# The first attention's projection as seven half-size products instead of eight

## The chip, the cores and the metric

The kernel runs on one core of a Trainium2 chip. The metric is the device time of one launch in microseconds, less is better. One profiled execution of the kernel before gives the rows that the text reads.

## The reference

Sixteen batches of a graph with 1024 nodes and 256 features go through two layers. Cut to what matters:

```python
h = maximum(layernorm(x), 0)
# layer 0
out = relu(h @ mlp1_w + mlp1_b)                 # [1024, 512]
residual = out
hf = out @ W_fc                                  # [1024, 512]: the projection that is changed
e = leaky_relu(f1[:, None] + f2[None, :], 0.2)   # f1 = hf @ a_fc[:512], f2 = hf @ a_fc[512:]
out = elu(elu(softmax(e) @ hf)) + residual       # dense attention, no mask
out = relu(out @ mlp2_w + mlp2_b)                # [1024, 256]
residual = out
out = elu(gat(out, adj, W_hand, a_hand)) + residual   # masked attention "a"
x = x + relu(out)
# layer 1
h = maximum(layernorm(x), 0)
x = x + relu(gat(h, adj, W, a, slope=0.01))      # masked attention "b"
```

All data is float32. The projection is, per batch, a product of 1024 x 512 by 512 x 512.

## The kernel before, in words

A batch's 1024 nodes are eight row tiles of 128. The activations `resT` are held with features on the partitions, in four blocks of 128 features; `wfc_sb` holds W_fc in two halves of 256 output columns, each with one more column that gives f1 or f2. `Dense.project(t, g)` (L754 to L767) multiplies row tile t by half g: four products of 128 x 128 weights by 257 columns are accumulated in one PSUM bank (L762), ScalarE copies the bank into `h_nat` (L764), and for half 0 GpSimd takes the f1 column out and writes ones in its place (L766, L767). Sixteen such calls make a batch.

The first attention has no mask, and is done without a 1024 x 1024 matrix for all batches but part of the first: the nodes are ranked by f2 (`rank`), their rows of `h_nat` scattered to DRAM in that order (`scatter`, GpSimd's indirect DMA), read back (`read_sorted`), and running sums made in both directions (`sum_before`, `sum_behind`). The sums are written as tables, each node gathers its row by its f1 (`gather`), and `share` and `mean` make the result `hp` of it. `merge` (L1001) transposes `hp` on TensorE and applies the two elu, `merge_end` adds it to `resT`, `mlp2` multiplies by mlp2_w. The two masked attentions (`Masked`: "a" and "b" in tile names) build 128 x 256 weights on VectorE (L667) in a ring of eight tiles with the tag "att", and multiply them (L677).

Engines work in the order of the program. That order is written out: `at(name, lo, hi, steps)` gives each step a nominal time, `SHIFT` moves single steps, and at the end all steps are sorted by that time and issued. TensorE, VectorE, ScalarE and SyncE take their instructions in that order, and GpSimd's are chained in it too, the scatters in between free among themselves. A period of 142 nominal units stands for one batch; `base_of(b)` is where batch b's begins. Several batches are in flight: while batch b is in its second masked attention, batch b + 1 ends its first one and batch b + 2 is projected. `dense_rows` places half 1 of the projection, `dense_begin` half 0 with the columns, the ranks and the scatters.

Tiles come from rings. `mm_psum` has four banks, `bc_psum` one tile of two banks, `tr_psum` two banks. The tag "seq" has two large buffers, taken in turn by `h_nat`, the sorted rows `xs`, the running sums `tt` and the two halves of the gathered rows `got`. A tile that is taken waits until the last user of its buffer is done.

## Time and profile before

| | |
|---|---|
| median of 3 runs | 2252.64 us (2251.83 to 2252.95) |
| the profiled execution | 2251.37 us |
| its span, first to last instruction | 2249.6 us |
| granted TensorE clock | 0.998 |
| LDWEIGHTS of the projection (L762) | 2048, 189 ns each |
| copies of its banks (L764, ScalarE) | 256 |
| HBM read and written | 226.88 MB and 126.29 MB |

A row of a group names line, engine, operation and tiles, then how many, the busy time in us and the mean length of one in ns, and the idle time of its engine just before, with what ended it. PE is TensorE's matmul, PEld its weight load, DVE VectorE, ACT ScalarE, POOL GpSimd, SP SyncE. A row of a stage (A:B) has the stage's length and then the busy time and number of instructions of PE, PEld, DVE, ACT and POOL. A row of waits has the us in total, how many, and the longest.

### The profile page before, as it was taken

What the parts mean: (1) busy time and instruction counts of PE and PEld (TensorE: products, weight loads), DVE (VectorE), ACT (ScalarE), POOL (GpSimd) and SP (SyncE); (2) the same over time, 40 slices, a digit from 0 to 9 for tenths busy, and PEclk for the clock granted to TensorE, in tenths of its full rate; (3) what the DMA queues carried; (4) which work ended last, traced back from release to release, by engine and by line L of the source; (5) the groups of instructions that cost most, each with busy time, mean ns of one, the idle gap of its engine ahead of it and who ended that gap; (6) DMA issues with size and microseconds to landing.
All of it is one profiled execution on the core that took longest, in us unless ns stands there. A gap on an engine that the chain in (4) does not pass through costs nothing.

```text
span 2249.6 us, 31025 instructions
## 1 busy us (share of the span) xinstructions
PE 2207.2 (98%) x9754; PEld 1723.4 (77%) x9754; DVE 1643.1 (73%) x4535; ACT 1259.6 (56%) x2797; POOL 954.4 (42%) x1212
## 2 busy tenths in 40 slices
PE   7999999999999999999999999999999999999997
PEld 5767777787877878787787877878787787877776
DVE  7677676777867678776776867677786776858765
ACT  5355745547365564756557375564746557365542
POOL 1163425263452536425263452636435263543620
PEclk9999999999999999999999999999999999999999
DMA  5568466675766757566685666757566585645700
GB/s 197 159 175 196 114 208 154 186 183 148 197 123 200 187 168 190 137 196 148 192 191 147 189 127 194 188 177 189 130 205 144 185 197 153 164 125 169 178 22 28
DMA packets 263870, 368.95 MB, mean 164 GB/s; under 512 B 124352, under 2 KB 175880, under 8 KB 259600
## 3 DMA queue, kind: packets, MB, share of 16 engines
q1 hardware_dynamic: 217088, 202.72, 31.9%
q0 software_dynamic: 45952, 163.99, 28.9%
q8 instruction: 80, 1.31, 0.3%
q14 instruction: 94, 0.77, 0.1%
q10 hardware_dynamic: 656, 0.17, 0.0%
HBM read 226.88 MB, written 126.29 MB: 157 GB/s over the span
## 4 chain that ended last, share of the span: by engine, by line
PE 75%; DVE 6%; DMA 2%; POOL 2%; ACT 1%; issue 1%; POOLq 0%; DVEq 0%; ACTq 0%; SPq 0%
PE oa L677 17%; PE h L762 16%; PE ob L677 14%; PE m L1024 8%; PE m L748 6%; PE pa L614 4%; PE pb L614 3%; PE hpT L1006 2%; DMA got<-coarse,k 2%; DVE attb L667 1%; PE carry L918 1%; PE on L1038 1%; PE nt L536 1%; DVE stats L516 1%; DVE hp L959 1%
## 5 line engine op out<-in xcount | busy, mean ns | idle before, releaser
L677 PE MATMUL ob<-hmb,attb 128*128 128x257 f32 x2048 | 463.9, 380 | 2.2 <-DVE attb L667 1.9
L762 PE MATMUL h<-wfc_sb,resT 128*128 128x257 f32 x2048 | 462.8, 379 | 0.0
L677 PE MATMUL oa<-hma,atta 128*128 128x258 f32 x2048 | 459.9, 382 | 1.8 <-DVE atta L667 1.5
L677 PEld LDWEIGHTS ob<-hmb,attb 128*128 128x128 f32 x2048 | 383.9, 190 | 67.2 <-issue 12.3
L677 PEld LDWEIGHTS oa<-hma,atta 128*128 128x128 f32 x2048 | 384.8, 190 | 59.3 <-DVE atta L667 2.9
L762 PEld LDWEIGHTS h<-wfc_sb,resT 128*128 128x128 f32 x2048 | 380.1, 189 | 59.1 <-issue 7.4
L705 POOL TENSOR_TENSOR posa<-posa,onat 128x256 f32<-128x256 f32 x118 | 106.7, 904 | 546.1 <-ACT posa L693 487.6
L667 DVE SCALAR_TENSOR_TENSOR attb<-rowsb,qwdb,edge 128x256 f32<-128x256 f32 (+1 forms) x536 | 292.1, 563 | 34.6 <-PE ob L677 28.6
L667 DVE SCALAR_TENSOR_TENSOR atta<-rowsa,qwda,edge 128x256 f32<-128x256 f32 (+1 forms) x520 | 257.3, 524 | 51.4 <-DMA rowsa<-row_a 35.6
L934 POOL DMA_INDIRECT got<-coarse,k x124 | 203.4, 1640 | 90.9 <-DMA got<-fine,k 56.6
L748 PE MATMUL m<-hT,w_sb 128*128 128x512 f32 x512 | 236.6, 596 | 1.9 <-ACT rb L719 1.1
L1024 PE MATMUL m<-resT,w_sb 128*128 128x512 f32 x512 | 228.3, 593 | 1.0 <-POOL resT L1017 1.0
L719 ACT ACTIVATE rb<-ob,recb 128x256 f32<-128x256 f32 x128 | 58.5, 474 | 274.9 <-DVE recb L717 248.9
L1017 POOL TENSOR_TENSOR resT<-resT,e 128x512 f32<-128x512 f32 x128 | 165.5, 1295 | 104.9 <-DVE e L1016 96.7
L692 ACT ACTIVATE ea<-oa,reca 128x256 f32<-128x256 f32 x128 | 60.3, 471 | 248.1 <-DVE reca L689 228.7
L934 POOL DMA_INDIRECT got<-fine,k x124 | 126.7, 1022 | 128.5 <-DVE hpd L999 41.9
L1024 PEld LDWEIGHTS m<-resT,w_sb 128*128 128x128 f32 x512 | 94.5, 190 | 102.4 <-issue 93.5
L748 PEld LDWEIGHTS m<-hT,w_sb 128*128 128x128 f32 x512 | 94.2, 191 | 89.0 <-issue 74.7
L822 POOL DMA_INDIRECT sorted<-hnat,place x128 | 128.6, 1004 | 53.9 <-DVE place L815 33.0
L764 ACT COPY hnat<-h 128x257 f32<-128x257 f32 x256 | 90.8, 367 | 104.1 <-PE h L762 101.6
L845 ACT ACTIVATE junk<-r,fs 128x1024 int8<-128x1024 f32 x124 | 142.6, 1150 | 0.9 <-POOL fs L766 0.6
L1016 DVE SCALAR_TENSOR_TENSOR e<-hpT,e 128x512 f32<-128x512 f32 x128 | 87.9, 688 | 53.2 <-ACT e L1010 53.0
(195 smaller groups left out, 3391.2 us busy)
## 6 DMA issues: line engine op xcount, KB each, us to landing
xs<-sorted SPq DMA_DIRECT2D x32, 1028.0 KB
fine<-tt SPq DMA_DIRECT2D x32, 1026.0 KB
fine<-xs SPq DMA_DIRECT2D x32, 1026.0 KB
x<-in_x_dram SPq DMA_DIRECT2D x16, 1024.0 KB
xn<-in_x_dram SPq DMA_DIRECT2D x15, 1024.0 KB
out_dram<-x SPq DMA_DIRECT2D x28, 512.0 KB
hT<-xn SPq DMA_DIRECT2D x416, 32.0 KB
coarse<-carry SPq DMA_DIRECT2D x32, 256.5 KB
```

Source lines behind the costliest of these rows:

```text
L614: nc.tensor.matmul(ps[:, :2 + F], lhsT=hT[:, c, t * P:(t + 1) * P], rhs=self.w_sb[:, c, 0, :], start=(c == 0), stop=(c == FC - 1))
L667: nc.vector.scalar_tensor_tensor(a_t[:, :n * P], self.rows[:, i], self.qwd[:, 1, j:j + 1], edge[:, j, i], op0=OP.max, op1=OP.mult)
L677: nc.tensor.matmul(self.out[t][:, :F + self.ONES], lhsT=self.att[t0, j][:, (t - t0) * P:(t - t0 + 1) * P], rhs=self.hm[:, j, 2:2 + F + sel ...
L705: adder.tensor_add(pos, pos, o_nat[:, t, :])
L748: nc.tensor.matmul(ps, lhsT=w1_sb[:, kc, c * P:(c + 1) * P], rhs=piece(kc, h), start=(kc == 0), stop=(kc == FC - 1))
L762: nc.tensor.matmul(ps[:, :F + 1], lhsT=self.resT[:, kc, t * P:(t + 1) * P], rhs=wfc_sb[:, kc, g, :], start=(kc == 0), stop=(kc == HC - 1))
L764: nc.scalar.copy(self.h_nat[:, t, g, :], ps[:, :F + 1])
L822: made = nc.gpsimd.indirect_dma_start(out=sorted_d[self.b % 2], out_offset=bass.IndirectOffsetOnAxis(ap=self.place[:, t:t + 1], axis=0), i ...
L845: nc.scalar.activation(junk, self.r2, AF.Sign, bias=self.fs[:, 0, t:t + 1], accum_out=self.signs[:, t:t + 1])
L934: nc.gpsimd.indirect_dma_start(out=got[u // n][:, u % n, :], out_offset=None, in_=(coarse_d if coarse else fine_d)[self.b % 2][:, :], in_o ...
L1017: nc.gpsimd.tensor_add(dst, dst, e)
L1024: nc.tensor.matmul(ps, lhsT=w2_sb[:, kc, c * P:(c + 1) * P], rhs=self.resT[:, kc, h * HALF:(h + 1) * HALF], start=(kc == 0), stop=(kc == H ...
```

## The change

The projection C = A B is cut into halves in all three dimensions, and the four blocks of C are made from seven products of half size instead of eight (Strassen's method in Winograd's form). A11, A12 are the upper 512 rows with feature blocks 0, 1 and 2, 3; A21, A22 the lower 512 rows. The sums of weight blocks are made once at the start (`seven_weights`, on GpSimd): the buffers of `wfc_sb` are overwritten by them, `wfc_more` holds two more, and B21 itself goes to DRAM and is loaded in each batch into two tiles of the attention ring. The sums of activation blocks are made per row tile, two on VectorE and two on GpSimd, also in that ring. Products 1, 6, 5 and 3 of a row tile accumulate in one PSUM bank, which is copied after each of them; product 7 of two row tiles goes to the two banks of `bc_psum` and is added to two blocks by `add_pair`; products 2 and 4 go to a bank each and are added by VectorE.

```diff
+    wfc_more = const.tile([P, 2, 2, F + 1], F32, name="wfc_more")
+    wfc_d = dram.tile([P, 2 * (F + 1)], F32, name="wfc_d")
+    def seven_weights():
+        top, low = slice(0, 2), slice(2, HC)
+        b11, b12, b21, b22 = [wfc_sb[:, k, g, :] for k in (top, low) for g in range(2)]
+        nc.sync.dma_start(wfc_d.rearrange("p (k f) -> p k f", k=2), b21)
+        nc.gpsimd.tensor_sub(wfc_more[:, 1], b22, b12)
+        nc.gpsimd.tensor_sub(b12, b12, b11)
+        nc.gpsimd.tensor_sub(wfc_more[:, 0], b22, b12)
+        nc.gpsimd.tensor_sub(b21, b21, wfc_more[:, 0])
...
+    def att_tile(name):
+        return big.tile([P, F + 1], F32, tag="att", name=name, bufs=ATT)
...
-        def project(self, t, g):
+        def sums_of(self, u, which):
...
+            a11, a12 = self.resT[:, 0:2, one], self.resT[:, 2:HC, one]
+            a21, a22 = self.resT[:, 0:2, two], self.resT[:, 2:HC, two]
+            t = self.s[which, u] = att_tile(f"s{which}_{self.b}_{u}")[:, :PAIR].rearrange(
+                "p (k n) -> p k n", k=2)
+            if which == 1:
+                nc.vector.tensor_add(t, a21, a22)
+            elif which == 2:
+                nc.vector.tensor_sub(t, self.s[1, u], a11)
+            elif which == 3:
+                nc.gpsimd.tensor_sub(t, a11, a21)
+            else:
+                nc.gpsimd.tensor_sub(t, a12, self.s[2, u])
+        def load_b21(self):
+            self.b21 = [att_tile(f"b21_{self.b}_{k}") for k in range(2)]
+            for k in range(2):
+                nc.sync.dma_start(self.b21[k], wfc_d[:, k * (F + 1):(k + 1) * (F + 1)])
+        def multiply(self, ps, lhs, rhs, start):
+            for k in range(2):
+                nc.tensor.matmul(ps, lhsT=lhs[:, k, :], rhs=rhs[k], start=start and k == 0,
+                                 stop=k == 1, skip_group_check=True)
+        def step(self, i, u):
...
-            ps = mm_psum(f"h_{self.b}_{t}_{g}")
-            for kc in range(HC):
-                nc.tensor.matmul(ps[:, :F + 1], lhsT=self.resT[:, kc, t * P:(t + 1) * P],
-                                 rhs=wfc_sb[:, kc, g, :], start=(kc == 0), stop=(kc == HC - 1))
-            nc.scalar.copy(self.h_nat[:, t, g, :], ps[:, :F + 1])
-            if g == 0:
-                nc.gpsimd.tensor_copy(self.fs[:, 0, t:t + 1], self.h_nat[:, t, 0, F:])
-                nc.gpsimd.memset(self.h_nat[:, t, 0, F:], 1.0)
+            a = {1: lambda: self.resT[:, 0:2, one], 2: lambda: self.resT[:, 2:HC, one],
+                 3: lambda: self.s[4, u], 4: lambda: self.resT[:, 2:HC, two],
+                 5: lambda: self.s[1, u], 6: lambda: self.s[2, u], 7: lambda: self.s[3, u]}[i]()
+            h = self.h_nat
+            if i in (1, 6, 5, 3):
+                if i == 1:
+                    self.chain[u] = mm_psum(f"h_{self.b}_{u}")
+                ps = self.chain[u][:, :F + 1]
+                self.multiply(ps, a, b, i == 1)
+                t, g = {1: (u, 0), 6: (u + TH, 0), 5: (u + TH, 1), 3: (u, 1)}[i]
+                nc.scalar.copy(h[:, t, g, :], ps)
+            elif i == 7:
+                if u % 2 == 0:
+                    self.pair = bc_psum(f"h7_{self.b}_{u}")
+                self.multiply(self.pair[:, u % 2 * HALF:u % 2 * HALF + F + 1], a, b, True)
+            else:
+                ps = mm_psum(f"h{i}_{self.b}_{u}")[:, :F + 1]
+                self.multiply(ps, a, b, True)
+                t = u if i == 2 else u + TH
+                nc.vector.tensor_add(h[:, t, 0, :], h[:, t, 0, :], ps)
+                nc.gpsimd.tensor_copy(self.fs[:, 0, t:t + 1], h[:, t, 0, F:])
+                nc.gpsimd.memset(h[:, t, 0, F:], 1.0)
+        def add_pair(self, u):
+            ps = self.pair.rearrange("p (u f) -> p u f", u=2)[:, :, :F + 1]
+            for g in (1, 0):
+                dst = self.h_nat[:, TH + u:TH + u + 2, g, :]
+                nc.vector.tensor_add(dst, dst, ps)
```

The tiles for the carries and for the lines sent to DRAM lose their own ring of two ("carry") and move into the two buffers of "part", which the means use:

```diff
-            carry = work.tile([P, K], F32, tag="carry", name=f"carry_{self.b}_{s}", bufs=2)
+            carry = work.tile([P, K], F32, tag="part", name=f"carry_{self.b}_{s}")
...
-        line = work.tile([NT, P], F32, tag="carry", name=name, bufs=2)
+        line = work.tile([NT, P], F32, tag="part", name=name)
```

The steps get new places: five of the seven products stand where half 1 stood (`dense_rows`), products 2 and 4 where half 0 stood (`dense_begin`), and nearly all of `SHIFT` is new. "mid" are the batches 1 to 12 in the order's own count. The rows that the prediction works with:

```diff
+        for lo, u, i in ((84, 0, 3), (84.5, 1, 3), (86.2, 0, 1), (86.3, 0, 2), (87.4, 1, 1),
...
+            at("dense_rows1", t0 + lo, t0 + lo, [partial(d.sums_of, u, i)])
+        for lo, i, u in ((85.3, 1, 0), (86.2, 1, 1), (87.1, 7, 0), (88, 7, 1), (89.2, 6, 0),
+                         (90.2, 6, 1), (91.2, 1, 2), (92.2, 1, 3), (93.4, 5, 0), (94.4, 5, 1),
+                         (95.6, 3, 0), (96.6, 3, 1), (98, 7, 2), (99, 7, 3), (100, 6, 2),
+                         (101, 6, 3), (103.6, 5, 2), (104.6, 5, 3), (107, 3, 2), (108, 3, 3)):
+            at("dense_rows2", t0 + lo, t0 + lo, [partial(d.step, i, u)])
+        for lo, u in ((96, 0), (106, 2)):
+            at("dense_rows3", t0 + lo, t0 + lo, [partial(d.add_pair, u)])
+        at("dense_rows4", t0 + 107.5, t0 + 107.5, [d.load_b21])
+    def late_steps(d):
+        return [partial(d.step, i, u) for i in (2, 4) for u in range(TH)]
...
+        late = late_steps(d)
+        at("dense_begin5", t0 - 31, t0 - 28, late[:2])
+        at("dense_begin6", t0 - 22, t0 - 10, late[2:])
+        scatters(d, t0 - 16, t0 - 2)
...
-    "mid dense_sums1": (-47.98,),
+    "mid dense_rows1": (-11, -7.9, -15.5, -14.8, -19.6, -16.9, -6.5, -11.2, 0, 0, -25, -21.2,
+        -29.1, -11.8, -18.8, -11.8,),
+    "mid dense_rows2": (-5.94, -4.6, -5.6, 0, -7, -7.3, -11.8, -12.7, -10.2, -7.9, 0, 0, 3.3, 2.4,
+        -17.7, -9, -17.8, -4.8, -13.2, -6.5,),
+    "mid dense_rows4": (-10.9,),
+    "mid dense_begin5": (0, -9.8,),
+    "mid dense_begin6": (-9.13, -10.2, -24.2, -26.2, -17.12, -27.3,),
```

In the first two batches the same steps come from `early_steps` and `late_steps`, and `seven_weights` stands behind the weight columns in the start. For one batch, the zero of `dense_begin` lies 142 nominal units behind that of `dense_rows`.

## The prediction

> **What bounds the kernel now.** I read the busy rows of the page first, then the chain of waits in a middle batch, then what TensorE waited for, then the groups that the change touches.
>
> ```profile
> span 2249.6 us, 31025 instructions
> PE 2207.2 (98%) x9754; PEld 1723.4 (77%) x9754; DVE 1643.1 (73%) x4535; ACT 1259.6 (56%) x2797; POOL 954.4 (42%) x1212
> ...
> L762 PE MATMUL h<-wfc_sb,resT 128*128 128x257 f32 x2048 | 462.8, 379 | 0.0
> ```
>
> The reader is to see that PE is busy 98% of the span, and that the group to be changed (L762) has 2048 rows for 16 batches x 64 products: one fp32 product is two PE instructions.
>
> The chain that ended last, in order of time, gives the true price of one instruction and the period:
>
> ```profile
> 1051.16 6.94 PE h L762 x32
> ...
> 1185.39 6.94 PE h L762 x32
> ```
>
> 6.94/32 = 217 ns from one to the next; the 379 ns of the group are its length with the drain, 162 ns of which the next instruction covers. The same piece returns after 134.23 us: the batch period. In between, in 1175 to 1309.3 us, the stages show PE busy in 133.9 of 134.3 us, DVE 98.9, ACT 76.7, POOL 60.3. Over the long middle, and in what PE waited for from 400 to 1850 us:
>
> ```profile
> 250.00:2030.00 1780.00, 1775.96 (x7777) 1384.89 (x7776) 1317.53 (x3585) 1029.50 (x2301) 808.57 (x1025) 1.00 0.64 170
> ...
> PE m L748 <- ACT rb L719: 1.1, 2, 0.8
> PE hpT L1006 <- DVE hp L959: 0.5, 2, 0.3
> ```
>
> Column two is PE busy: 4 us idle in 1780. So a PE instruction that is taken away from the middle is worth its 217 ns, until something else becomes late. The idle rest is at the ends: 11.1 us before the first transpose, some 6 us up to 250, and 21 us from 2030 on, 10 of them behind the last matmul.
>
> Here a rule speaks against the change. The Trainium skill, "Perfetto Trace Analysis", section Identifying the Most-Contended Engine, says that matmul busy time does not measure PE's headroom and that the busy share of weight loads does. That share is 77%, so by the rule PE keeps 23% in hand, something else would set the time, and the removal would be worth nothing. The row decides: pieces of 32 instructions at 217 ns with no gap, and 1.6 us of waits in 1450. I take the 217.
>
> **The change part by part.** *Removed.* 7 half products for 8: per batch 56 instead of 64 products, 16 instructions less; in all 256 x 217 ns = 55.6 us, 3.48 us per batch. The shape (257 columns, 128 weights) stays, so the price does. All of it lies on PE's path in the middle: -55.6.
>
> *Added on DVE, per batch.* Eight sums of two SBUF tiles of 256 columns (sums_of 1 and 2); nearest rows:
>
> ```profile
> L723 DVE TENSOR_TENSOR x<-x,rb 128x256 f32<-128x256 f32 x128 | 52.1, 424 | 11.7 <-ACT rb L719 11.7
> L1016 DVE SCALAR_TENSOR_TENSOR e<-hpT,e 128x512 f32<-128x512 f32 x128 | 87.9, 688 | 53.2 <-ACT e L1010 53.0
> L705 POOL TENSOR_TENSOR posa<-posa,onat 128x256 f32<-128x256 f32 x118 | 106.7, 904 | 546.1 <-ACT posa L693 487.6
> ```
>
> 8 x 0.42 = 3.4. Eight additions of a 257-column bank onto h_nat (steps 2 and 4): between 0.38, the fastest L723, and 0.69; by width 0.43, 3.4 again. Four add_pair operations of 514 columns at L1016's 0.69: 2.8. Sum 9.6 us per batch, 153 in all. DVE goes to 98.9 + 9.6 = 108.5 of a period of about 131 us, 83%: beside PE, not in front of it.
>
> *Added on POOL.* Eight subtractions of 256 columns at 0.78 to 0.90 (L706, L705): 6.7 us per batch, 108 in all, on an engine at 60 of 134. *ACT* copies 16 banks of 257 columns per batch, as before: nothing. *SP* gets two b21 loads of 131 KB per batch, 4.2 MB beside 369; the first product that uses them stands some 6 nominal units behind their issue. Cover gone, a late b21 would hold PE for the landing, at worst a few us per batch.
>
> A second rule speaks against it. The same skill, "SBUF — State Buffer", section Who interferes with whom: a DVE instruction with two SBUF inputs and a POOL instruction that reads SBUF shut each other out for a whole instruction. This trace agrees: L723 has a median of 418 ns and a maximum of 994, and a 256-column L667 took 1.50 us beside a POOL addition of 1.28. By the rows' means the sum is the 9.6 above, since they already hold such waits; if each new POOL subtraction shut out DVE for its whole length, 6.7 more, and DVE would stand at 115 of 131, 88%. Either way PE stays the bound; I take the rows and keep the rest for the range.
>
> *New waits on PE.* The four products 1, 6, 5, 3 of a row tile accumulate in one bank that ACT copies after each, so the next of them waits for the copy: 162 ns of drain, 373 ns of copy (L764's median), two hops of about 40 ns: 0.62 us. Behind the waiting instruction stands all of PE, which works in order; ACT's own queue, if it holds an activation of 0.6 to 0.7 us, adds that. Twelve such handoffs per batch, 192 in all. What covers them is the order. With the new SHIFT a middle batch has, as (product, tile) at nominal times: (1,0) 79.4, (1,2), (1,3), (7,0) 81.5, (1,1), (6,0) 82.2, (6,2), (6,1) 82.9, (5,0) 83.2, (5,2) 85.8. Between two products of one tile stand at least two others, each four instructions or 0.87 us, so 1.7 against 0.62: nothing, if ACT is less than a microsecond behind. One place has no cover: (3,3) at 101.5 is followed at once by (2,1), whose bank in the ring of four is the one that tile 3's chain gives up by that copy. 0.6 us in each of the 12 middle batches: +7. Lower end 0, upper end 1.3 per batch.
>
> *Sums ahead of their products.* Sum 1 of tile 0 stands at 70.7, sum 2 at 71.5, their products 5 and 6 at 83.2 and 82.2; DVE has room there (in 1160 to 1190 us it is busy about 15 of 30, POOL 15). The ring of eight attention tiles that they use is free between the last product of the second attention, near 67, and the next weights. Nothing.
>
> *Shared ring.* Carries and the three sent lines move into the two "part" buffers of the means. A mean whose buffer's last user is a line would wait for that line's write; in the middle batches the second attention's line (99.3) stands among the means of the second half (99.1 to 100.9). No row gives the landing; from the send of the dense line at 1199.67 to the first rank at 1205.4 is 5.7 us, but that holds a broadcast read too. Bounds 0 and some 3 us per batch on ACT, behind which the means and PE's last transposes stand; those are at 103.3 and later with late products between, so I take 0.
>
> *Start.* seven_weights is four POOL operations of 514 columns, 4 x 1.3 (L1017's 1.295 for 512) = 5.2 us, behind the weight columns which end at 20.4 us, while the first product of h starts at 27: just in time. But DVE is busy 35 of the 40 us from 30 to 70, and batch 0 puts 9.6 us into them; masks can move later. Between 0 and 8 lost: +2.
>
> *Moved.* Nearly every step has a new place: scatters end some 9 nominal units earlier, sums begin a little later, sums_begin returns behind the sorted read in the middle batches, so POOL no longer stands waiting (123.5 us over 14 batches at L881) for a mean; loads of x go earlier on SP, in whose order the table writes and sorted reads stand. The gathers' wait on DVE (100 us at L946) is the chain that this order must keep: I count 0, and its loss is a rival below. The last 220 us hold no projection; the new order there can give or take a few us: 0.
>
> Sum against the profiled execution (2251.37 us, 1.8 outside the span): -55.6 + 7 + 2 = -46.6, hence 2204.8. The median of the runs shown is 1.3 above that execution: **2206**.
>
> **The rivals.** *The gather chain becomes the bound.* Scatter, sorted read, sums, tables, gathers and means are DMA and DVE latencies that don't shrink. For it: at 1191.7 the last mean ends and PE's transposes of it start 0.3 us later, so PE meets it just in time. Against it: five of seven products now stand early and only two late, so after the last projection there is more PE work to cover the chain, not less. If two thirds of the gain is waited away in 13 batches, 30 us come back: about 2236; a third gives 2221.
>
> *The handoffs are not covered (slower).* If ACT runs behind its copies, PE stops at each. All 192 exposed cost 119 us and give 2316; it decides from 55.6/0.62 = 90 exposed, about 5.6 of 12 per batch. With 140 exposed: 2197 + 87 = 2284. For it: ACT is busy 14.4 of 17.6 us in the very stretch (1175 to 1192.6) where these copies fall, and there a bank that was full at 1187.1 was copied at 1189.67, 2.5 us late. Against it: the order spaces them, and four banks at once carry four chains.
>
> *Better than the sum.* The bank wait is hidden and the new order mends part of the 27 us of idle ends: 2190 to 2198.
>
> *It doesn't do what it says.* L762's successor would show over 1792 instructions; the text of the code gives 56 products, so I leave it no chance.
>
> **How the numbers follow.** My forecast (2198 to 2216) 0.64, better 0.10, the chain 0.13 (of it 0.01 within 0.2%), the handoffs 0.13 (0.02 within 0.2%). About 0.2%, 4.5 us, is what a measurement of this kernel can tell from no change. So faster 0.85, same 0.03, slower 0.12. The range from 2190 to 2236 leaves out the handoffs, the worst third of the chain's case and a little below: under 0.2.
>
> **What would show it.** Right: 1792 instructions of h at 217 ns in the chain, a period near 131 us, DVE near 83% in it, PE busy near 2150 us, waits of PE on ACT's copy of a bank about 0.6 us once per batch. Wrong: PE waiting for "hp" or "got" for microseconds each batch (chain), for ACT's hnat copy many times per batch (handoffs), or a period that stays at 134.

## The result: slower by 0.3%, and the profile after

The changed kernel takes 2258.97 us (median of 20 runs, 2256.26 to 2264.93), the kernel before 2253.04 (20 runs, 2251.14 to 2255.87): a ratio of 1.0029, 95% interval 1.0022 to 1.0036. Predicted were 2206 and a gain. The profiled execution took 2259.29 us against 2251.37.

The page of the changed kernel; where it stood at L667, L677 and L762 the code now stands at L708, L718 and L820:

```profile
span 2257.5 us, 31185 instructions
...
PE 2183.9 (97%) x9498; PEld 1668.4 (74%) x9498; DVE 1797.5 (80%) x4855; ACT 1267.5 (56%) x2797; POOL 1066.4 (47%) x1344
...
L718 PE MATMUL oa<-hma,atta 128*128 128x258 f32 x2048 | 477.1, 385 | 18.9 <-DVE atta L708 14.9
...
L708 DVE SCALAR_TENSOR_TENSOR atta<-rowsa,qwda,edge 128x256 f32<-128x256 f32 (+1 forms) x520 | 250.7, 523 | 76.1 <-DMA rowsa<-row_a 72.0
...
L820 PE MATMUL h<-wfc_more,s 128*128 128x257 f32 x512 | 127.2, 381 | 0.9 <-DVE s L807 0.8
L820 PE MATMUL h<-wfc_sb,s 128*128 128x257 f32 x512 | 125.6, 383 | 0.9 <-ACT hnat L845 0.9
```

The removal is there: PE has 256 instructions less, and the new products cost what the old ones did. DVE rose by 154 us (153 predicted), POOL by 112 (108). But PE's busy time fell by only 23 us, and the span grew by 8. The stage that the prediction showed as 1775.96 of 1780 us busy, and what PE waited for over the whole execution (us in total, times, longest):

```profile
250.00:2030.00 1780.00, 1747.37 (x7561) 1336.68 (x7559) 1434.83 (x3812) 1026.75 (x2286) 892.54 (x1123) 1.00 0.63 172
```

```profile
PE oa L718 <- DVE atta L708: 14.9, 29, 0.6
PE hpT L1100 <- DVE e L1110: 14.5, 12, 1.2
...
PE m L1118 <- POOL resT L1111: 4.6, 5, 2.3
PE oa L718 <- ACT hma L702: 2.5, 6, 0.6
...
PE h L820 <- ACT hnat L845: 0.9, 2, 0.5
```

The two large waits before:

```profile
PE hpT L1006 <- DVE e L1016: 1.5, 3, 1.1
PE oa L677 <- DVE atta L667: 1.5, 3, 0.7
```

The list is too short all the same: a busy PE instruction counts with its drain of 162 ns, so a stall below that leaves no idle time. I therefore worked stalls out from the trace: for each PE instruction the time from its start to the next start, less the usual step of that kind. By that, PE stalled for 36.8 us before and 104.6 after:

| stretch | before | after |
|---|---|---|
| 0 to 200 us | 11.0 | 28.4 |
| 200 to 800 | 7.0 | 22.2 |
| 800 to 1600 | 2.5 | 26.8 |
| the rest | 16.3 | 27.2 |

That is 67.8 us of new stalls for 55.6 us of instructions removed; the 12.2 that result stand beside 7.9 measured, and the 4 between are this working's error. By name, from 200 us on: "oa" +35 us, some 2.9 per batch; "hpT" +12; the projection "h" +3. Of the 39 us that "oa" stalled after, DVE's weights "atta" ended 20, copies and scalings on ScalarE 11, and 7 have no name.

The period, from one transpose of "exta" to the next, in the timeline of the changed kernel:

```profile
1107.90 0.27 PE L532 MATMUL extpsa<-ident,exta 128*128 128x128 f32 x1
...
1242.98 0.27 PE L532 MATMUL extpsa<-ident,exta 128*128 128x128 f32 x1
```

That is 135.1 us; most intervals of the middle are 135.3, against 134.2 before. PE's work per period fell to 130.7 (134.2 less 3.5), as the prediction had it, and 4.5 us of stalls came in (26.8 over 5.9 periods). In the profiled executions the first such transpose comes at 182.8 us instead of 170.8 (+12.0), the twelve periods after it add 5.0, and the stretch behind them is 473.3 instead of 482.4 (-9.1): together the 7.9. Of the 256 removed instructions 32 stood at the start, 192 in the twelve periods and 32 behind them (6.9, 41.7 and 6.9 us). So beside the removal the start lost 19 us, the periods lost 47, and the last stretch won 2.

The start has a part that is not a wait. The third value from the end of a row of a stage is the granted clock; before, then after:

```profile
140.00:150.00 10.00, 7.46 (x28) 4.10 (x28) 7.23 (x14) 8.06 (x15) 8.93 (x13) 1.00 0.26 101
150.00:160.00 10.00, 9.60 (x29) 4.49 (x28) 5.36 (x10) 8.23 (x16) 8.14 (x10) 1.00 0.71 260
```

```profile
140.00:150.00 10.00, 7.79 (x28) 5.47 (x28) 5.38 (x14) 7.99 (x14) 7.96 (x10) 0.66 0.80 131
150.00:160.00 10.00, 7.62 (x16) 2.98 (x15) 6.45 (x14) 7.56 (x13) 7.55 (x7) 0.83 0.68 185
```

PE ran at half its clock for 10.2 us there, in two pieces behind stalls of 2.3 and 2.5 us, and a product of 512 columns took 850 ns from start to start instead of 429. That costs up to 5.1 us, nearly as much as the whole difference between the kernels.

**Where atta becomes late.** All times from here on are counted from that transpose ("ext"), in the same middle batch: 1229.57 us before, 1242.98 after. The names: "rowsa" is the row of 1024 values that the first masked attention needs on all partitions, "atta" the weights that DVE makes of it and "oa" PE's products with them; "exta" is a maximum and minimum on DVE that precedes them, and ext its transpose.

| event | before | after |
|---|---|---|
| score line to PE (line_ps) | -31.36 | -27.44 |
| last rank ready | -6.72 | -0.84 |
| read of sorted rows xs issued | -3.33 | +4.19 |
| read of rowsa issued | +4.35 | +3.56 |
| first running sum tt | +3.53 | +11.49 |
| first weight atta | +9.00 | +8.07 |
| last product oa | +41.68 | +45.19 |

The ranks, and with them the sort, are six us later; so SP issues the row for the masked attention first and the sorted rows behind it, the other way round than before. SP's queue before and then after:

```profile
1226.24 0.82 SPq L866 DMA_DIRECT2D xs<-sorted  x2
1233.92 0.32 SPq L652 DMA_DIRECT2D rowsa<-row_a  x1
```

```profile
1246.54 0.34 SPq L693 DMA_DIRECT2D rowsa<-row_a  x1
1247.18 0.81 SPq L961 DMA_DIRECT2D xs<-sorted  x2
```

And DVE in the timeline, before and after (start, us, what, idle before):

```profile
1233.10 0.49 DVE L894 TENSOR_SCALAR tt<-xs,bd 128x513 f32<-128x513 f32 x1 [1.55 <-ACT bd L885]
1233.63 2.33 DVE L896 SCALAR_TENSOR_TENSOR tt<-xs,bd,tt 128x513 f32<-128x513 f32 x3
1238.57 1.28 DVE L667 SCALAR_TENSOR_TENSOR atta<-rowsa,qwda,edge 128x256 f32<-128x256 f32 x3 [2.61 <-DMA rowsa<-row_a]
```

```profile
1251.05 2.86 DVE L708 SCALAR_TENSOR_TENSOR atta<-rowsa,qwda,edge 128x256 f32<-128x256 f32 x7 [6.21 <-DMA rowsa<-row_a]
1254.47 0.49 DVE L989 TENSOR_SCALAR tt<-xs,bd 128x513 f32<-128x513 f32 x1 [0.56 <-ACT bd L980]
1255.00 2.33 DVE L991 SCALAR_TENSOR_TENSOR tt<-xs,bd,tt 128x513 f32<-128x513 f32 x3
```

Before, four running sums (2.75 us) fill the time in which DVE waits for the row. After, DVE idles 6.2 us there, and the same sums stand among the weights, where DVE has no room. From +9 to +42, before and then after (PE is the second value, DVE the fourth):

```profile
1238.57:1271.57 33.00, 33.00 (x157) 28.29 (x156) 31.37 (x74) 14.53 (x35) 10.24 (x12) 1.00 0.67 177
```

```profile
1251.98:1284.98 33.00, 31.24 (x143) 25.61 (x142) 32.06 (x73) 14.18 (x37) 8.04 (x10) 1.00 0.55 167
```

DVE had 1.6 us to spare there before, less than the 2.75 that were put in. PE, which multiplies those weights at once, waits.

**The wait of hpT.** DVE, then PE, in the timeline of the changed kernel:

```profile
1198.46 1.47 DVE L807 TENSOR_TENSOR s<-s,resT 128x256 f32<-128x256 f32 x1 [0.70 <-POOL s L811]
1199.85 0.68 DVE L1110 SCALAR_TENSOR_TENSOR e<-hpT,e 128x512 f32<-128x512 f32 x1
```

```profile
1198.87 0.60 PE L1100 MATMUL hpT<-ident,hp 128*128 128x128 f32 x4
1200.68 0.63 PE L1100 MATMUL hpT<-ident,hp 128*128 128x128 f32 x4 [1.21 <-DVE e L1110]
```

A sum for a product (s, tile 3) stands on DVE ahead of the end of a merge (e), and takes 1.47 us. PE's transposes of the next merge need the bank that e gives up, and wait 1.2 us, in each middle batch.

### The profile page after: what moved, and what is told of

It reads as the page before. It is cut to its first block, busy times and chain, and to the rows that moved or that the text cites. A ratio compares the mean times of both kernels' runs of the same rounds, so it can differ in the third digit from the quotient of the medians.

```text
span 2257.5 us, 31185 instructions
## 1 busy us (share of the span) xinstructions
PE 2183.9 (97%) x9498; PEld 1668.4 (74%) x9498; DVE 1797.5 (80%) x4855; ACT 1267.5 (56%) x2797; POOL 1066.4 (47%) x1344
## 5 line engine op out<-in xcount | busy, mean ns | idle before, releaser
L718 PE MATMUL oa<-hma,atta 128*128 128x258 f32 x2048 | 477.1, 385 | 18.9 <-DVE atta L708 14.9
L718 PE MATMUL ob<-hmb,attb 128*128 128x257 f32 x2048 | 474.1, 380 | 1.3 <-DVE attb L708 0.8
L718 PEld LDWEIGHTS oa<-hma,atta 128*128 128x128 f32 x2048 | 381.7, 190 | 101.1 <-DVE atta L708 26.4
L718 PEld LDWEIGHTS ob<-hmb,attb 128*128 128x128 f32 x2048 | 381.0, 190 | 67.7 <-issue 16.4
L708 DVE SCALAR_TENSOR_TENSOR atta<-rowsa,qwda,edge 128x256 f32<-128x256 f32 (+1 forms) x520 | 250.7, 523 | 76.1 <-DMA rowsa<-row_a 72.0
L746 POOL TENSOR_TENSOR posa<-posa,onat 128x256 f32<-128x256 f32 x118 | 98.2, 832 | 437.4 <-ACT posa L734 436.9
L708 DVE SCALAR_TENSOR_TENSOR attb<-rowsb,qwdb,edge 128x256 f32<-128x256 f32 (+1 forms) x536 | 263.0, 514 | 11.2 <-PE ob L718 8.7
L1029 POOL DMA_INDIRECT got<-coarse,k x124 | 201.3, 1623 | 46.5 <-issue 35.4
L792 ACT ACTIVATE resT<-m,b_sb 128x512 f32<-128x512 f32 x128 | 87.6, 686 | 145.2 <-PE m L789 145.1
L1103 ACT ACTIVATE e<-e 128x512 f32<-128x512 f32 x128 | 80.3, 627 | 95.0 <-DVE e L1102 90.7
L820 PE MATMUL h<-wfc_more,s 128*128 128x257 f32 x512 | 127.2, 381 | 0.9 <-DVE s L807 0.8
L820 PE MATMUL h<-wfc_sb,s 128*128 128x257 f32 x512 | 125.6, 383 | 0.9 <-ACT hnat L845 0.9
```

Source lines behind the costliest of these rows:

```text
L708: nc.vector.scalar_tensor_tensor(a_t[:, :n * P], self.rows[:, i], self.qwd[:, 1, j:j + 1], edge[:, j, i], op0=OP.max, op1=OP.mult)
L718: nc.tensor.matmul(self.out[t][:, :F + self.ONES], lhsT=self.att[t0, j][:, (t - t0) * P:(t - t0 + 1) * P], rhs=self.hm[:, j, 2:2 + F + sel ...
L746: adder.tensor_add(pos, pos, o_nat[:, t, :])
L792: nc.scalar.activation(self.resT[:, c, h * HALF:(h + 1) * HALF], ps, AF.Relu, bias=b1_sb[:, c:c + 1])
L820: nc.tensor.matmul(ps, lhsT=lhs[:, k, :], rhs=rhs[k], start=start and k == 0, stop=k == 1, skip_group_check=True)
L1029: nc.gpsimd.indirect_dma_start(out=got[u // n][:, u % n, :], out_offset=None, in_=(coarse_d if coarse else fine_d)[self.b % 2][:, :], in_o ...
```

## The experiments

A ratio is to the kernel before on the same chip, with its 95% interval. Numbers in `SHIFT` move single steps, in nominal units.

### What a PE instruction is worth

**e1**, the kernel before with 8 of its 64 products left out:

```diff
-            for kc in range(HC):
+            some = 2 if g == 0 and t < TH else HC
+            for kc in range(some):
```

> The kernel before, in its old places, with 8 of the 64 projection products of each batch left out (group 0, tiles 0 to 3 add up only two of their four parts of the contraction; half of it is left out there). It takes from TensorE exactly what the change takes, 16 instructions x 217 ns = 3.47 us per batch, and adds nothing to any other engine. If TensorE alone set the period before, as the prediction had it, 16 x 3.47 = 55 us come off: about 2197, period near 130.7. If a second loop (vectors, gathers, transfers) stood just behind TensorE, the period stays near 133 to 134 and the time at 2235 to 2253; then no saving on TensorE could have brought the predicted time in these places.

Measured: 2225.41 us, 0.9889 [0.9874, 0.9904]. With the same 55.6 us of PE instructions gone, and nothing added or moved, only 25 came off.

```profile
PE pa L614 <- ACT oT L1028: 13.9, 12, 1.5
```

The wait in that row, all of PE, is 1.2 us in each of 12 batches: the period falls from 134.2 to 132.1, not to 130.7. Outside the twelve periods 14 us of the removed instructions brought next to nothing: the first ext comes at 172.2 (170.8 before), the end gains 3, and PE ran at half its clock for 10.2 us at the start, as in the changed kernel. A dense PE row did not mean that the full price can be had. These eight products are of half 0; no run left out others.

**e4**, the changed kernel with product 2 of each tile done twice (the expectation says step 3, the code doubles product 2), so that PE has its old load again:

```diff
+                if i == 2:
+                    self.multiply(ps, a, b, True)
```

> The kernel after, with the product of step 3 of each tile multiplied twice into its bank (the second time from zero, so the value is the same): 8 products = 16 instructions x 217 ns = 3.47 us more on TensorE per batch, nothing elsewhere. If TensorE still sets the period, +55 us, about 2314. If a loop with 4.7 us of TensorE stalls per batch sets it, as the trace after suggests, the addition is mostly taken up by those stalls: +5 to +30, 2264 to 2290.

Measured: 2313.25 us, 1.0277 [1.0263, 1.0291]. All of the 55.6 came on top (+54 by the medians, +56 by the ratios), and the stalls stayed (29.0 us in 800 to 1600, 26.8 without). PE's new stalls are no slack that work could fill: they lie in series with its work.

### The wait of hpT

**e8**, the changed kernel with the merge's end ahead of that sum on DVE:

```diff
-    "mid merges2": (2.7, -5.7, 7.7, 0, 10.06, 7.9, 8.7, 8.6,),
+    "mid merges2": (-2.5, -5.7, 7.7, 0, 10.06, 7.9, 8.7, 8.6,),
```

> The kernel after, where in the middle batches the end of the first merge (e_0_0) stands ahead of the sum s2 of tile 3 on VectorE, not behind it. In the kernel after that sum waits 0.7 us for GpSimd and takes 1.47 us itself, and the next transposes hpT wait 1.2 us for e. If that wait is on the path, 1 to 1.4 us per batch in some 10 batches come off: 2244 to 2250. If the wait is made up elsewhere (something else ends as late): within 3 of 2259.

Measured: 2249.98 us, 1.0001 [0.9993, 1.0009]: level with the kernel before, and 6 us better than the change by the two ratios (9 by the medians, which are of different chips). In 800 to 1600 us, the changed kernel and then e8:

```profile
PE hpT L1100 <- DVE e L1110: 6.0, 5, 1.2
```

```profile
PE hpT L1100 <- DVE e L1110: 0.5, 2, 0.2
```

The wait of the weights (6.6 us in both lists) did not move. So one misplaced sum is 6 us or a little more. e8 has the same 10.2 us at half clock at its start.

### Late running sums

**e13** is e1, in the old places, with only the first four running sums moved behind the first weights:

```diff
-    "mid dense_sums4": (-3.79, -4.33, -5.22, -5.77, -3.99,),
+    "mid dense_sums4": (0.8, -0.4, -1.6, -2.8, -3.99,),
```

> As e1_fewer (the kernel before in its old places, 8 products per batch left out), with the first four running sums tt due 4.6 us later in the middle batches, so that they stand behind the row's first weights atta on VectorE instead of ahead of them; the sorted rows are read as early as before. Late sort theory: the last oa comes 1.5 to 3 us later than 41.7 after extpsa, and 15 to 30 us are added: 2240 to 2255 against e1_fewer's 2225. If the running sums have slack there: 2223 to 2230.

Measured: 2254.61 us, 1.0016 [1.0009, 1.0024]; e1 was at 0.9889. Moving four sums costs 29 us (both ran 10.2 us at half clock at the start); the last oa goes from +41.68 to +44.17, and the new wait of after is there in 800 to 1600 us:

```profile
PE oa L677 <- DVE atta L667: 5.1, 11, 0.8
PE oa L677 <- ACT rb L719: 2.9, 6, 0.5
```

**e15** takes the work from the other side: e8, with the first four sums of batch 2 and later on one column of 513.

```diff
+            if r < TH and self.b > 1:
+                row, tt = row[:, K - 1:], [t[:, K - 1:] for t in tt]
```

> As e8_e_first, with the first four running sums tt of each batch from the third on made on one column of 513 (the other 512 columns are left out of these sums and set to a constant by GpSimd beforehand); every instruction keeps its place. VectorE has about 2.3 us less between the row and the last weights of each batch. Late sort theory: the last oa comes 2 to 2.5 us earlier (+43 instead of +45.4) and 2 to 2.5 us per batch come off: 2220 to 2230 against e8_e_first's 2250. If TensorE waits there for something other than VectorE's work: within 5 of 2250.

Measured: 2239.27 us, 0.995 [0.9936, 0.9964], 11 below e8. The wait of oa on atta in 800 to 1600 falls from 6.6 to 3.7 us, the last oa comes 1.35 earlier (1.0 in the mean of ten batches). The four sums take 0.87 us instead of 2.75, and of these 1.9 us per batch about half comes off the time.

Where the sums stand behind the first weights one relation held, worked out from the traces: the last oa comes 33.7 us after the first tt, whenever that is (+45.19 - 11.49 here; 33.7 also in e4, e5, e6, e8 and e10; 32.9 in e13, which has the old places). With the sums in their old place it came at +41.68 even where the first atta came between 8.9 and 10.4: there PE's own work set it.

Five attempts to mend it by order follow; none did.

**e11** fills the idle time ahead of the row with other DVE work (on e8, two statistics of the next input):

```diff
-    "mid first_norm3": (-37.94, -9.3, 0, 0, -23.6, -10.3, 0, -5.13,),
+    "mid first_norm3": (-62.6, -9.3, 0, 0, -65.3, -10.3, 0, -5.13,),
```

> As e8_e_first, with the statistics of two tiles of the next batch's input (2 x 0.6 us on VectorE) moved out of the stretch in which TensorE waits for each atta, to just ahead of it, where VectorE sits idle for 6 us until rowsa lands. If VectorE's pace in that stretch is what TensorE waits for, 0.8 to 1.2 us per middle batch come off: 2237 to 2243 against e8_e_first's 2250. If not, 2248 to 2252.

Measured: 2250.64 us, 1.0002 [0.9993, 1.001], as e8. The first tt stood at +11.79: DVE then waited 1.3 us for xs.

**e14** (on e8) issues the second half of xs later, on ScalarE's queue, so that the first might land sooner:

```diff
+            if h == 0 and self.b >= 2:
+                self.read_half(1, nc.scalar)
```

> As e8_e_first, nothing left out, with one transfer moved: of the two reads of sorted rows (1 MB each) only the first, which the first four running sums need, is issued on SP behind the row's read; the second is issued on ScalarE's queue behind the weights bd of the first half, so that the two no longer share the DMA engines. Late sort theory: the first half lands 2.5 to 3.5 us earlier, tt starts at about +8.5 us after extpsa instead of +11.7, the last oa follows at tt + 33.7 = +42.2 or at TensorE's own 41.7, and 2 to 3 us per batch come off in some 12 batches: 2214 to 2228 against e8_e_first's 2250. If the pace is set by the whole of VectorE's work behind the row, and not by when the sums start, or if the second half then comes too late for the fifth sum: 2244 to 2256.

Measured: 2267.48 us, 1.0069 [1.0055, 1.0083]. ScalarE began on the first half 7.2 us after its issue, against 6.9 with both issued at once: the second does not hold up the first. The fifth sum came late instead.

**e12** puts the order around the sort back: columns, ranks and sorted read earlier, the first four sums ahead of the weights, eight attb behind the ranks, and e8's edit. Its core:

```diff
-    "mid dense_begin8": (-1.6,),
+    "mid dense_begin8": (-3.5,),
-    "mid dense_sums4": (-4.9, -6.12, -7.37, -8.6, -4.4, -4.8, -5.5, -4.1,),
+    "mid dense_sums4": (-12.500, -13.700, -14.900, -16.100, -4.4, -4.8, -5.5, -4.1,),
```

> The whole change, nothing left out, with the order around the sort put back in the middle batches: scores copied and sent before the second MLP's first product, all ranks ahead of exta, the eight weights attb of the first pair of tiles behind the ranks (four of them in VectorE's idle time before rowsa lands), xs read ahead of rowsa, the first four running sums tt ahead of the first atta, and e8_e_first's order of e and s2. Late sort theory: ranks end 5 to 6 us before extpsa, tt starts at +4 to +6 us instead of +11.5, the last oa comes at +42 to +43 instead of +45.2, and the period falls by 2 to 3 us below e8_e_first's 134.4: 2218 to 2232. If the last oa stays 33.7 us behind tt, it comes as early as TensorE's own 41.7 allows, the same numbers. If the pace is set by something else: 2245 to 2260. If the ranks do not end early enough, xs meets the row in the DMA engines: 2265 to 2290.

Measured: 2274.11 us, 1.011 [1.0094, 1.0125]. The sums did come early (+5.39), but the row came late behind the 2 MB of xs (its read went out at +6.82 instead of +3.56, first atta +11.1), and the last oa stayed at +45.23.

**e16** (on e8) moves the last four backward sums out of the stretch, the table's write behind them:

```diff
-    "mid dense_sums7": (-5, -5.4, -6.8, -6.1, -4.3, -5.6, -5, 1.4,),
+    "mid dense_sums7": (-5, -5.4, -6.8, -6.1, 11.550, 10.663, 10.375, 10.188,),
```

> As e8_e_first, nothing left out, with the last four of the eight backward sums (4 x 0.74 us on VectorE) due 8 to 16 us later in the middle batches, two of them behind the last weight atta, and the table write and the carry that follow them behind them. Theory as before: VectorE has 1.5 to 3 us less ahead of the last weights, the last oa comes 1.5 to 3 us earlier, 15 to 30 us come off: 2220 to 2235, faster than both kernels. If the gathers, which start up to 8 us later, then hold up the means: the gain is lost to DVE den waiting for got, 2245 to 2270.

Measured: 2315.75 us, 1.0293 [1.0279, 1.0307]. The last oa went to +42.53, so DVE's sums do set it, but the price came back: a gather, which needs the table that is now written later, starts late with all of GpSimd behind it. The row gives no name to what ended the idle time; that it was the table is inferred. GpSimd's gather, then PE's wait in 800 to 1600 us:

```profile
1328.63 1.10 POOL L1029 DMA_INDIRECT got<-fine,k  x1 [5.86 <-issue]
```

```profile
PE m L789 <- ACT rb L760: 17.6, 5, 4.8
```

The additions "ea" stood behind that gather, x behind ea on DVE (26.3 us of waits), and PE behind both. Behind PE's long waits the clock fell too: 41.0 us at half clock, against 10.2 in e8, up to 15 of the 66 us lost.

**e17** moves them less, and the gathers behind the last ea:

```diff
-    "mid early_gathers1": (5, 5.01,),
+    "mid early_gathers1": (7.0, 7.01,),
```

> As e8_e_first, nothing left out, with the last four backward sums moved behind the next to last weight atta (up to 3 us less vector work ahead of it; a little earlier than in e16_sums_behind), and the first gathers behind the last two sums ea on GpSimd. If the only loss of e16_sums_behind was what stood behind the waiting gathers: the last oa near +43, period 132 to 133.5, 2225 to 2242, faster than both kernels. If the gathers themselves are then too late for the means (DVE den waits for got): 2245 to 2275.

Measured: 2277.74 us, 1.0112 [1.0095, 1.0129]. Last oa +43.86; now the next normalisation stands behind the gathers (DVE's waits in 800 to 1600 us):

```profile
DVE hn L567 <- POOL rstd L563: 37.1, 12, 6.6
```

### Why the sort is late

**e3** shrinks the added DVE work: the bank additions and add_pair only on their last column, the other 256 left out.

```diff
-                nc.vector.tensor_add(h[:, t, 0, :], h[:, t, 0, :], ps)
+                nc.vector.tensor_add(h[:, t, 0, F:], h[:, t, 0, F:], ps[:, F:])
```

> The kernel after, in its places, with the late additions of steps 2 and 4 and the additions of pairs made on one column of 257 (the other 256 columns are left out of these sums), so that VectorE has about 5 us less per batch and every instruction, wait and handoff stays. Vector theory: the period falls from 135.8 by 2 to 5 us, toward TensorE's 131.1; 2190 to 2225. Order theory: within 8 us of 2259. Handoff theory (banks given back late): only the 0.2 us per batch that the trace shows, 2254 to 2259.

Measured: 2258.22 us, 1.003 [1.002, 1.004]. DVE loses 58 us of busy time and nothing comes of it: the last rank stays at -0.84. At this place the amount of added work does not matter: the rank stands behind "exta", for which DVE waits 1.9 us.

**e2** issues the sorted read ahead of the row again:

```diff
-    "mid dense_begin8": (-1.6,),
+    "mid dense_begin8": (-2.5,),
```

> The kernel after, with one place put back: the read of the sorted rows (xs) is issued ahead of the read of the row (rowsa) on SP again, as before. Order theory (the new places make the loss): xs lands 1.8 us earlier in each batch, and if that read stands on the closed loop, some 13 x 1.8 = 23 us come off, about 2236. Vector theory (the added 9.6 us of VectorE work per batch make the scatter and the sums late): the scatter itself lands at about the same time, and the row waits behind it, so 0 to 5 us, 2254 to 2259. It may also be slower by 5 if the row then waits on the scatter.

Measured: 2294.82 us, 1.0192 [1.0178, 1.0206]. The read waits for the scatters, and the row, whose read goes out at +3.55 (+3.56 without this edit), lands behind it:

```profile
DVE atta L708 <- DMA rowsa<-row_a: 57.6, 6, 10.1
```

**e5** also puts the last ranks ahead of exta:

```diff
-    "mid dense_begin4": (4.7, -1.9, 3.5, -5.7, -4.8, -4.2, -8.1, -13.2,),
+    "mid dense_begin4": (4.7, -1.9, 1.8, -5.7, -4.8, -4.2, -8.1, -13.2,),
```

> The kernel after, where in the middle batches the last of the eight ranks stands ahead of the extreme exta on VectorE (it stood behind it, and behind exta's 1.9 us wait), and the read of the sorted rows (xs) ahead of the read of the row (rowsa) on SP. The last scatter then lands about 2 us earlier, before the row is ready, so that xs no longer holds up rowsa as it did in e2_sorted_first (atta began 11.5 us after extpsa there, 8.1 in the kernel after). Theory of the late sort (the sorted rows come after the row's weights instead of before, and 5.5 us of running sums are pushed into the stretch in which TensorE waits for each atta): the period falls by 1.5 to 3 us in some 9 middle batches, 2230 to 2246. Theory that the pace of that stretch is set by something else: within 5 of 2259.

Measured: 2287.8 us, 1.0166 [1.0152, 1.018]. The last rank came at -2.95, two us earlier; row and xs were in flight together, and the first atta went to +11.18.

**e6** takes columns, score line, ranks and scatters three units earlier (the columns' line of it), and **e7** adds e3's narrow additions to it:

```diff
-    "mid dense_begin1": (-3.7,),
+    "mid dense_begin1": (-6.4,),
```

> As e5_rank_first, and the column of scores is copied and sent (columns, send) one step earlier in the middle batches, ahead of the second MLP's first product on TensorE (3.5 us), with ranks and scatters due 3 us earlier. Late sort theory: the row r lands 3 us earlier; as VectorE is full from there to the ranks, 1 to 3 us of that reach the scatter; 2215 to 2240, lower than e5_rank_first. If VectorE's own load (late additions) holds the ranks, it is no better than e5_rank_first.

> As e6_line_first, with the late additions and the additions of pairs made on one column of 257 (256 columns are left out of them), 5 us less on VectorE per batch, all of it ahead of the ranks. If the late sort comes from both the place of the row and the added vector work, the ranks end 3 to 5 us earlier than in e6_line_first and it is faster by 10 to 30: 2195 to 2225. If the vector work has no part in it (as e3_narrow_adds alone would say), it equals e6_line_first within 5.

Measured: 2331.18 us, 1.0361 [1.0347, 1.0376], and 2316.14, 1.0294 [1.028, 1.0308]. The last rank came at -10.06 and the stalls of oa halved (17.6 to 8.5 us in 800 to 1600), but the ranks now stand ahead of the merges' ends on DVE. In e6 PE ran 64.9 us at half clock, in e7 51.2 (10.2 in the changed kernel), which is up to 27 and 20 us of their loss. All of e6:

```profile
PE m L1118 <- POOL resT L1111: 54.5, 17, 4.3
```

**e10** is e7 with those steps only one unit earlier:

> As e7_line_narrow (scores sent one step earlier, additions on one column of 257, the other 256 left out, xs read ahead of rowsa), but the ranks due only 1 us earlier, so that they stand behind the merges' ends on VectorE instead of ahead of them; e7_line_narrow's 4.3 us wait of the second MLP for resT goes. Late sort theory: the last place is ready 5 us before extpsa, xs is read before the row needs the DMA engines, the wait of TensorE for atta falls from 1.9 us per batch to 1 or less as it did in e6_line_first and e7_line_narrow: 2235 to 2252. If the sort is still not early enough, xs and the row meet in the DMA engines as in e5_rank_first: 2275 to 2295.

Measured: 2280.97 us, 1.0135 [1.012, 1.0151]: last rank -3.71, but the sorted read at -0.02 stands ahead of the row (read at +6.77), and the first atta comes at +10.65.

**e9** loads the kernel with old places: e1 with additions of h + 0 x product on DVE where the products are made, close in number and width to those of the change:

```diff
+                nc.vector.scalar_tensor_tensor(dst, src, 0.0, dst, op0=OP.mult, op1=OP.add)
```

> As e1_fewer (the kernel before in its old places, 8 products per batch left out), with about 9 us of VectorE work added per batch at the projection's own steps: 7 operations of 257 columns beside group 1, 8 that read the product's bank and 4 of 514 columns beside group 0; they put back the values that are there (h + 0 x), so they only cost time. It carries the change's TensorE saving and its VectorE load without its places, its sums on GpSimd or its chains. If the added vector work is what eats the saving, 2245 to 2262 instead of e1_fewer's 2225. If the new places and the late column of scores eat it, 2222 to 2232.

Measured: 2393.23 us, 1.0638 [1.0624, 1.0653], 168 above e1. In 800 to 1600 us, DVE's wait and PE's:

```profile
DVE hnat L769 <- ACT hnat L766: 34.5, 36, 1.9
```

```profile
PE pa L614 <- ACT oT L1041: 23.0, 6, 3.8
```

Some 8 us of additions per batch (DVE's busy time is 124 us above e1's) and 5.7 of waits for copies (34.5 over 6) stood on DVE ahead of work that PE needs; the period went from 132.1 to about 143. Behind PE's long waits the clock fell to half for 78.5 us in all, against 10.2 in e1: up to 34 of the 168. Such work is anything but free there. The change carries more of it (154 us) and stands at 2259; that its new places avoid this price, and pay with the late sort, is argued and not shown by a run.

## Why the prediction was wrong, point by point

| term | predicted | what the runs show |
|---|---|---|
| 256 instructions removed | -55.6 | -25 alone in the old places (e1); the old load put back is +54 (e4) |
| DVE +9.6 per batch, "beside PE" | 0 | amount right (154 us in all), verdict wrong |
| sums ahead of products | 0 | +6: one of them ahead of e on DVE (e8) |
| moved steps | 0 | late running sums: 2.2 us per batch (29 us, e13), 2.9 per batch of stalls here |
| product handoffs, bank wait | +7 | +3 of stalls from 200 us on, at another place |
| start | +2, at most 8 | +19 (12 longer with 7 of PE work gone), up to 5 of it the clock |
| end | 0 | -2 (9 shorter, 7 of them PE work gone) |
| POOL, ACT, b21 loads, shared ring | 0 | nothing of size (PE waited 0.7 us for b21, ACT 0.9 us for the ring) |

Two steps failed. The first is "a PE instruction that is taken away from the middle is worth its 217 ns, until something else becomes late". The second half of that sentence was not priced. 4 us idle in 1780 told that nothing came too late for PE; it did not tell by how little. e1 shows that the next thing was right behind: at 2.1 us per batch of 3.5 the gain ends, and PE waits for the copy oT; that an earlier copy would bring the rest was not tried.

The second, which decides the sign, is "83%: beside PE, not in front of it", with "Moved: I count 0". DVE's share over a period says nothing of the stretch from ext to +42, where it was nearly full before (31.4 of 33 us), nor of its order. Four running sums of 2.75 us left a gap where they cost nothing for a stretch where they cost PE time; e13 shows it alone in the old places, e15 from the other side. The prediction looked at the moved steps only as a chain of gathers. That rival is refuted: over 800 to 1600 us DVE waited 46.5 us for the gathers before and 1.4 after, so the chain had more room than before.

"Nothing" for the sums was read from DVE's room in 1160 to 1190 us, a mean again. A 1.47 us instruction just ahead of one that PE waits for held PE up by 1.2 us per batch, of which e8 won back 0.5 to 0.7. The rule on SBUF access by DVE and POOL was weighed only as a share of DVE; half of these sums (L807, 64 of them) took 0.42 us or less, but their mean is 0.73, and a long one stood at this one place.

The slower rival, the handoffs, was the wrong mechanism: PE waited 0.9 us for the copies in all by the list of waits, some 3 us with what the drain hides. The one bank wait that was priced, product 2 behind product 3, shows no stall; product 5 of tile 0 behind product 6 of tile 1, which was counted as covered, stalls 0.2 us in each middle batch, as its bank's copy ended just before. The rule of the Trainium skill ("Perfetto Trace Analysis", Identifying the Most-Contended Engine) that judges PE's headroom by the busy share of weight loads (and by the share of peak), 74% after, would have given the nearer number, no gain, but not for its reason: e4 shows no headroom for added work.

Of the signs named, 1792 products at their old price and DVE near 83% came (650 of 800 us in the middle, 81%); the wait for a copied bank came once per batch at a third of its size; the period near 131 and PE busy near 2150 did not come. Of the signs of being wrong one came, the period that stays (135.3; 134 was named).

At the start the sums, additions and masks of batch 0 meet on DVE, busy 47.35 of 50 us in 50 to 100 (33.67 before), and PE waits for m (4.3 us), mask_ps (2.5) and b_ps (2.1). How the loss divides between these is argued from the trace. Two runs bear on it: in e3 the first ext comes at 182.6 with 8 us less of DVE work in the first 200, so the amount of bank additions and add_pair hardly matters there; and e1, which adds nothing anywhere, has the half clock at its start too. Two more things stay open: how much of the late sort comes from the order of the products (half 1, which carries a score column, now ends behind products 7, 5 and 3; after the score line PE has 16 instructions of h to go, 48 before) and how much from the added DVE work (e3 took 58 us of it away, and the ranks did not move); and whether an order exists that keeps e8's gain and has the sums back ahead of the row. No kernel that computes all of the reference beat the kernel before; e8 ties with it.

## What to carry to other kernels

A busy PE row priced added work well (e4) and removed work badly (e1): before counting a gain, look in the trace for how early each operand of PE came, for the margin of the second-latest is the end of the gain. Price work added to an engine "with room" by the instruction that it is put in front of, and by whether the stretch in question is full, not by the share of a period. When an order is written anew, compare event by event, from one anchor, what goes out ahead of what on each queue.

## What the hardware showed that was not expected

PE's busy time hid most of the stalls: busy fell by 23 us where 55.6 us of instructions had gone, since up to 162 ns between two instructions count as drain.

A long wait of PE cost twice. The granted clock fell to half in pieces of 3.4 to 10.2 us, 92 of them over these runs ahead of their last products, and each came within 7 us of a PE stall of 1.3 us or more; the kernel before had none above 1.44 us behind its first products, and no such piece. In e6 they came in nearly every middle batch, behind its stalls of 4.3 us. Not every long stall brought one.

A transfer moved late when a larger one had been issued before it; this is worked out from the DMA packets in the traces. In e2 the 0.5 MB row was read at +3.55, a microsecond behind the 2 MB of sorted rows; its packets moved from +8.95 to +11.04, when those of the sorted rows were nearly through (+3.46 to +9.79), and the first atta came 8.0 us after the read's issue, against 4.5 in the changed kernel. In e10 it was the 4 KB write of the row: issued at +1.76 as in the changed kernel, its packets moved at +5.4 instead of +2.5, with the sorted rows moving from +0.95 to +7.17, and the read of the row went out only at +6.77.

A sum of 256 columns on DVE took 1.47 us beside a GpSimd addition of 1.27, against 0.42 for its kind. And GpSimd sat idle for 5.86 us ahead of a gather, with everything behind it late (e16).
